# A graph-attention layer on one core: four overflow slots in place of seven, and seven more row tiles turned by VectorE instead of TensorE

## The chip, the cores and the metric

The kernel runs on one core of one Trainium2 chip. The metric is the device time of one launch in microseconds, and lower is better. The core's engines are TensorE (PE, matrix products), VectorE (DVE), ScalarE (ACT), GpSimd (POOL) and SyncE (SP); each takes its own instructions in the order in which they were queued. DMA queues belong to ScalarE, GpSimd and SyncE. PSUM is the memory that TensorE writes its results to.

## The reference

x is 2708 x 1024 in float32; adj is 2708 x 2708 with an edge at each place with chance 0.0014771, so a row has four edges on average. The weights are 1024 x 1024.

```
h   = relu(layernorm(x))
q   = h @ W_q.T + b_q;  k = h @ W_k.T + b_k;  v = h @ W_v.T + b_v
z   = (q @ k.T) / sqrt(1024) * adj
z   = where(z == 0, -10000, z)
out = x + relu(softmax(z, axis=1) @ v)
```

## The kernel before

**Two rewritings.** The kernel first forms M = W_q.T W_k / sqrt(1024), so that a score is (h_i M + b) . h_j and k is never formed. The values are summed as rows of h and multiplied by W_v afterwards. So there are two products of 2708 x 1024 by 1024 x 1024: the *q product* (h by M) and the *o product* (the weighted sums of rows of h by W_v). Only edges are scored and summed.

**Sorted tiles.** The 2708 rows are 22 tiles of 128 (the last has 20 rows). VectorE and ScalarE read adj, list up to 16 (`SLOTS`) neighbours of each row (`found`, `listed`) and count them (`counted`). Within tiles 0 to 7 and within tiles 8 to 21 the rows are sorted by their number of edges: `counts` prepares, `sort` has two small matmuls of TensorE, `put` writes the rows of the table `tab` to `tab_dram` in sorted order, and `reload` reads it back. From then on "tile t" is a sorted tile, and h is gathered by the table. Sorted tile t has K[t] slots, of which the first of each part (tiles 0 and 8, `HOSTS`) needs most, 15. Their first 8 (`WIDE`) slots stay with them; the rest goes to a shared spill tile (`SECOND`, number 21): its upper 64 partitions hold the slots 8 to 14 of the 64 longest rows of tile 0, its lower 64 those of tile 8, so `VK` is 7. The spill tile has scores and sums as a tile does; its sums go to `v_dram`, its sums of weights to `mass`, and each host adds them to its own (`m`, L904 on, and the last step of `sums`). Were a row longer than its slots, a general path at the end of the kernel would run.

**Units.** TensorE's work after M is a row of *units*: ten q pairs (units 0 to 9: tiles 0 and 1, 2 and 3, and so on), ten o pairs (units 10 to 19, in the order of the list `order`: tiles 6 and 5, 4 and 3, ...), and one single tile (`alone`, tile 8, the last of `order`). A pair of tiles is multiplied as a 2x2 block matrix with seven block products in place of eight. `blocks` (L711) makes the operands: a11, a12, a22 are transposed halves of the two row tiles; s1 = a22 + a21, s3 = a11 - a21, s2 = s1 - a11, s4 = a12 - s2 are sums of VectorE. `opened(n + 1)` issues unit n+1's products of a11 and of s1 inside unit n, ahead of unit n's last product (a22); `multiply(n, ...)` issues the other five and calls `after(0)` to `after(6)` between them. `after` is the place where all other work is put into the queues: unit n at step i is written (n, i).

**How a tile gets transposed.** In units up to 10 and in some later ones TensorE does it: `half_turned` (L415) makes four 128x128 transposes into PSUM, and ScalarE copies the half (L718) or VectorE uses it from PSUM. In the other way, called *faced* here, the rows are stored with the columns combed (ScalarE's copy L944 and a store to `u_dram`), read back by four quarter loads (`by_quarters`, L700), and VectorE turns 32x32 blocks in place (`faces`, L705); TensorE has no part in it. `faced_tiles` says which output tiles go this way:

```
if now < [unit - 2, 2] and unit <= len(q_pairs) + 4:
    faced_tiles.add(t)
```

that is, tiles whose sums are done early enough for their unit, in units up to 14. The single tile is transposed by TensorE (`turned`).

**The attention stream.** `attention` is a generator that hands out VectorE's long steps one by one, tile by tile in `order`, with the spill tile ahead of tile 0: `scores` (L863, one step for each slot: gathered rows of h times the rows of q, summed to one number), `weights`, and `sums` (L923, one step for each slot after the first; the first is an ACT copy, L912). `fill` queues gathers of h rows (L610, GpSimd) into eleven and later thirteen slots as they come free. `fetch` brings the q rows of a tile, called `pq`: for tiles 0 to 7 by a gather from `q_dram`, for the others by a plain load from `q_late` on SyncE's queue (L831, L833). `advance(share)` in `after` pulls some steps into VectorE's queue at each of the seven places of a unit; `share` (us by the kernel's own estimate of 1.3 for each long step) is 20.9/7, less 2.3/7 for each faced tile of the next unit.

**Order by hand.** `manual_schedule` fixes the order of ScalarE and VectorE (up to unit 3; after that VectorE's alone), and of GpSimd in two stretches. What goes where is written in `steps_at`, a list of short codes for each (unit, step): p = `counted` (ScalarE counts an adjacency tile), f and i = `found`, a = `apply` (normalise), k = `keep` (store h rows to `h_dram` and leave their sum for later), + = `owe` (four quarter additions of a tile to `hsum`, L298, on GpSimd), w = `put`, z and b = `reload`. The q pairs from unit 4 on gather their rows from `h_dram` (`load_rows`, "qr", L612); at (2, 5) the order in GpSimd's code is owe(8), owe(9), rows of unit 4, owe(10), owe(6), owe(7), rows of unit 5.

The functions that the diff touches, with the profile's line numbers:

## Time and profile before

| | before |
|---|---|
| median of 3 runs | 640.27 us (639.92 to 641.12) |
| the profiled execution's own time | 639.94 us |
| its span in the profile | 638.1 us |
| mean granted TensorE clock | 0.997 |
| busy: PE | 627.8 us (98%), 1651 instructions |
| busy: DVE | 522.4 us (82%), 1016 |
| busy: POOL | 360.2 us (56%), 383 |
| busy: ACT | 283.6 us (44%), 423 |
| moved by DMA | 176.96 MB, mean 277 GB/s |

The span is the time from the first to the last record of the profile; the execution's own time holds a little more. Busy time is what the profiler recorded for the engine's own instructions; a DMA that an engine issues is counted for the queue, except for the gathers and scatters of GpSimd, which have records of their own. In a row of the trace, "start duration engine line operation output<-inputs, shape" stand in this order, and the bracket at its end says how long the engine had been idle before it and what ended that.

### The profile page before, as it was taken

The page shows a single profiled execution, that of the slowest core. Times are in us where ns is not written, and L with a number is a line of the kernel's source. Part 1 is how long each engine was busy: PE and PEld are TensorE (multiplying, and loading weights), DVE is VectorE, ACT ScalarE, POOL GpSimd, SP SyncE. Part 2 cuts the span into 40 slices and gives each one's busy share as a digit, 9 for nine tenths or more (in the row PEclk, how much of TensorE's full clock was granted, in tenths as well). Part 3 has the DMA queues.
Part 4 walks back from the last instruction along what each step waited for, and adds up shares of the span by engine and source line. Part 5 has one row for each costly group of instructions (what it writes and reads, how often), then busy time and mean ns, then how long its engine had stood idle before and what let it go on. Part 6 is the DMA issues. An engine that isn't in the chain of part 4 may idle for free.

```text
span 638.1 us, 6156 instructions
## 1 busy us (share of the span) xinstructions
PE 627.8 (98%) x1651; PEld 317.9 (50%) x1651; DVE 522.4 (82%) x1016; ACT 283.6 (44%) x423; POOL 360.2 (56%) x383
## 2 busy tenths in 40 slices
PE   9999999999999999999999999999999999999994
PEld 5777766444444444444444444444444444444441
DVE  5999888997997625999888999999999889989121
ACT  3538985849667533424342144343342432333200
POOL 2639960885768357565651663476466878633311
PEclk9999999999999999999999999999999999999998
DMA  8999997598796439996798998999999999853631
GB/s 335 407 362 321 342 351 286 200 323 330 255 379 231 171 95 317 327 323 223 233 299 289 290 414 222 295 344 311 363 382 325 325 290 291 266 145 77 187 119 50
DMA packets 60192, 176.96 MB, mean 277 GB/s; under 512 B 9799, under 2 KB 15255, under 8 KB 59512
## 3 DMA queue, kind: packets, MB, share of 16 engines
q0 software_dynamic: 25136, 78.41, 39.4%
q1 hardware_dynamic: 29514, 78.61, 35.0%
q10 hardware_dynamic: 5502, 19.48, 7.8%
q8 instruction: 15, 0.25, 0.2%
q14 instruction: 25, 0.20, 0.1%
HBM read 145.65 MB, written 40.74 MB: 292 GB/s over the span
## 4 chain that ended last, share of the span: by engine, by line
PE 90%; issue 4%; POOL 2%; DMA 2%; DVE 1%; POOLq 0%; ACT 0%; ACTq 0%; DVEq 0%
PE ps L1010 40%; PE psy L1010 29%; PE ps_y L476 6%; PE ps_x L476 4%; PE ps_z L476 4%; PE pt L415 4%; POOL g L610 2%; DMA v_dram<-u 1%; DMA M<-h_dram,tab 1%; PE ps_y L511 1%; DVE junk L863 0%; PE ps_h L1218 0%; PE ps_v L594 0%; DVE u L923 0%; DVE s L722 0%
## 5 line engine op out<-in xcount | busy, mean ns | idle before, releaser
L610 POOL DMA_INDIRECT g<-h_dram,tab x94 | 120.2, 1278 | 79.9 <-DVE u L923 30.0
L1010 PE MATMUL psy<-wlow,s 128*128 128x512 f32 x320 | 144.0, 592 | 0.0
L1010 PE MATMUL ps<-M,a 128*128 128x512 f32 x320 | 144.0, 593 | 0.0
L863 DVE SCALAR_TENSOR_TENSOR junk<-g,pq 128x1024 uint8<-128x1024 f32 x93 | 113.8, 1224 | 13.4 <-DMA g<-h_dram,tab 10.4
L1010 PEld LDWEIGHTS ps<-M,a 128*128 128x128 f32 x320 | 59.7, 190 | 70.4 <-issue 69.1
L923 DVE SCALAR_TENSOR_TENSOR u<-g,coef,u 128x1024 f32<-128x1024 f32 x69 | 88.4, 1281 | 7.0 <-ACT u L912 5.8
L1010 PEld LDWEIGHTS psy<-wlow,s 128*128 128x128 f32 x320 | 59.6, 190 | 69.2 <-issue 69.0
L389 DVE FIND_INDEX8 at<-ones,adj 128x8 uint32<-128x685 f32 (+1 forms) x88 | 74.5, 864 | 0.0
L1010 PE MATMUL ps<-wlow,s 128*128 128x512 f32 x160 | 72.0, 593 | 0.4 <-DVE s L722 0.4
L1010 PE MATMUL ps<-M,s 128*128 128x512 f32 x160 | 72.1, 592 | 0.0
L1010 PE MATMUL psy<-wlow,a 128*128 128x512 f32 x160 | 72.0, 593 | 0.0
L368 ACT ACTIVATE sized<-adj 128x2708 uint8<-128x2708 f32 (+1 forms) x22 | 54.3, 2467 | 7.4 <-DMA adj<-in_adj_dram 6.1
L298 POOL TENSOR_TENSOR hsum<-hsum,x 128x256 f32<-128x256 f32 (+1 forms) x56 | 38.6, 732 | 26.2 <-DVE wlow L444 22.5
L1109 POOL DMA_INDIRECT y<-in_x_dram,tab x19 | 34.2, 1798 | 28.9 <-ACT y L1134 12.1
L1010 PEld LDWEIGHTS ps<-wlow,s 128*128 128x128 f32 x160 | 30.3, 190 | 38.9 <-issue 38.5
L1010 PEld LDWEIGHTS psy<-wlow,a 128*128 128x128 f32 x160 | 30.3, 190 | 38.5 <-issue 37.3
L1010 PEld LDWEIGHTS ps<-M,s 128*128 128x128 f32 x160 | 30.3, 190 | 38.1 <-issue 37.4
L808 POOL DMA_INDIRECT out_dram<-y,tab x21 | 27.4, 1306 | 32.0 <-DMA y<-in_x_dram,tab 15.8
L912 ACT ACTIVATE u<-g,coef 128x1024 f32<-128x1024 f32 x18 | 20.7, 1149 | 35.8 <-DVE coef L911 35.6
L276 ACT ACTIVATE x<-x,r 128x1024 f32<-128x1024 f32 (+1 forms) x22 | 25.9, 1232 | 6.6 <-POOL r L266 6.6
L722 DVE TENSOR_TENSOR s<-a,pt 128x512 f32<-128x512 f32 x30 | 19.2, 681 | 10.9 <-ACT a L718 10.9
L476 PE MATMUL ps_y<-wlow 128*128 128x512 f32 x64 | 27.6, 592 | 0.0
(251 smaller groups left out, 843.3 us busy)
## 6 DMA issues: line engine op xcount, KB each, us to landing
adj<-in_adj_dram SPq DMA_DIRECT2D x21, 1354.0 KB, 11.5
x<-in_x_dram SPq DMA_DIRECT2D x21, 512.0 KB, 8.2
h_dram<-x ACTq DMA_DIRECT2D x21, 512.0 KB, 7.4
q_late<-q SPq DMA_DIRECT2D x12, 512.0 KB, 5.1
pq<-q_late SPq DMA_DIRECT2D x12, 512.0 KB, 6.6
u_dram<-v ACTq DMA_DIRECT2D x10, 512.0 KB, 6.4
or<-u_dram SPq DMA_DIRECT2D x40, 128.0 KB, 7.0
M<-in_wv_dram SPq DMA_DIRECT2D x4, 1024.0 KB, 8.4
```

The source lines that it names most:

```text
L276: nc.scalar.activation(xs[i][:n], xs[i][:n], AF.Relu, bias=r[:n, 4, i:i + 1], scale=r[:n, 3, i:i + 1])
L298: small.append(nc.gpsimd.tensor_add(hsum[:n, cols], hsum[:n, cols], xt[:n, cols]))
L368: nc.scalar.activation(sized[:n], a[:n, :, :PW], AF.Abs, accum_out=total[:n, t:t + 1])
L389: nc.vector.max_index(at[:n, k - first_k, g, :], ones[:n, 0:8], a[:n, g, :])
L415: nc.tensor.transpose(pt[:, c, :], xt[:, k * P:(k + 1) * P], ident)
L476: mm = nc.tensor.matmul(bank, a_tile(o + H * a[0], a[1], i), b(o), start=first and o == 0, stop=(o == H - 1), skip_group_check=True)
L610: return nc.gpsimd.indirect_dma_start(out=dst, out_offset=None, in_=src, in_offset=off, bounds_check=N - 1, oob_is_err=False)
L808: to = nc.gpsimd.indirect_dma_start(out=out, out_offset=bass.IndirectOffsetOnAxis(ap=ptab.bitcast(U32)[:n, t, SLOTS:SLOTS + 1], axis=0), i ...
L863: chained(lambda: nc.vector.scalar_tensor_tensor(junk, g_of[t][s], 1.0, tq[t], op0=ALU.mult, op1=ALU.mult, accum_out=zall[:, t, s:s + 1]))
L923: chained(lambda: nc.vector.scalar_tensor_tensor(u, g_of[t][s], coef[:, s:s + 1], u, op0=ALU.mult, op1=ALU.add))
L1010: mm = nc.tensor.matmul(bank, a[:, c, :], b[:, c, :], start=False, stop=(c == 3), skip_group_check=True)
L1109: return nc.gpsimd.indirect_dma_start(out=y[:n], out_offset=None, in_=x, in_offset=off, compute_op=ALU.add)
```

## The change

The change has six parts.

1. **Four overflow slots.** `VK` is 4, and the spill tile holds each host's overflow in two pieces (`OVER`): for tile 0, slots 8 to 11 of its 48 longest rows on partitions 0 to 47 and slots 12 to 15 of its 8 longest on 48 to 55; for tile 8, 60 rows on partitions 56 to 115 and 12 on 116 to 127. The longer rows' second piece is added into the gathered first piece by an accumulating DMA, and `mass` has four columns.
2. **One q pair faced.** Pair 6 (`QFACED`, tiles 12 and 13) is gathered raw at (3, 3) into row tiles, combed by ScalarE and stored to `hq_dram` at (4, 2), and read back by quarters at (4, 3). (Steps are handed out by `after` at the end of a product, and the instructions' places in the engines' queues follow from the order lists and, for engines whose order is not fixed, from the scheduler.)
3. **More output tiles faced.** The condition admits units up to 15, and the units from 19 on and the single tile without regard to the time: pairs 5 and 9 of the output and tile 8. The single tile's rows are loaded at the end of unit 18 and turned by VectorE in one instruction.
4. **q rows by GpSimd.** The loads of `pq` from `q_late` are on GpSimd's queue.
5. **Load.** `share` is 22.0/7 before the last q unit, 18.2/7 in the two after that, 21.3/7 from there; the spill tile comes ahead of tile 3 instead of tile 0.
6. **Order.** At (2, 5) the rows of unit 4 are loaded ahead of all five `owe`; at (2, 3) the normalising and storing of tiles 8 to 10 comes ahead of counting p17; the second half's `put` is queued behind the last `root` of GpSimd instead of behind the last block product.

```diff
     HOSTS = (0, EARLY)
+    QFACED = (6,)
     SECOND = NT - 1
-    HP = P // 2
-    VK = K[0] - WIDE
-    assert K[0] == K[EARLY] and K[SECOND] == 0 and WIDE + VK <= SLOTS
+    VK = 4
+    OVER = ((48, 0), (8, 48)), ((60, 56), (12, 116))
...
-    mass = const.tile([P, 2], FT, name="mass")
+    mass = const.tile([P, 4], FT, name="mass")
+    nc.vector.memset(mass, 0.0)
...
-    for t in HOSTS:
-        nc.vector.memset(cap[:HP, t:t + 1], float(WIDE + VK))
+    for t, parts in zip(HOSTS, OVER):
+        for i, (rows, at) in enumerate(parts):
+            nc.vector.memset(cap[:rows, t:t + 1], float(WIDE + (i + 1) * VK))
...
             elif step[0] == "w":
-                with tc.issue_after((behind if first < EARLY else products)[-1].ins):
+                with tc.issue_after((behind if first < EARLY else rooted if first > EARLY else products)[-1].ins):
...
-        part = slice(HP, P) if lo >= EARLY else slice(0, HP)
-        loads.append((nc.gpsimd if lo >= EARLY else nc.sync).dma_start(
-            ptab[part, SECOND, 0:SLOTS + 1 - WIDE], src[0:HP, WIDE:SLOTS + 1]))
+        for i, (rows, at) in enumerate(OVER[lo >= EARLY]):
+            slot = WIDE + i * VK
+            loads.append((nc.gpsimd if lo >= EARLY else nc.sync).dma_start(
+                ptab[at:at + rows, SECOND, 0:SLOTS + 1 - slot], src[0:rows, slot:SLOTS + 1]))
+            if i and lo < EARLY:
+                loads.append(nc.sync.dma_start(ptab[at:at + rows, SECOND, SLOTS - WIDE:SLOTS + 1 - WIDE],
+                                               src[0:rows, SLOTS:SLOTS + 1]))
...
-                (2, 2): "p16", (2, 3): "p17 a8 k8 z", ...
+                (2, 2): "p16", (2, 3): "a8 k8 p17 z", ...
...
         if t == SECOND:
-            gather(tq[t][:HP], q_dram[:, :], t, SLOTS - WIDE, HP)
-            nc.sync.dma_start(tq[t][HP:], q_late[:HP, :])
+            rows = sum(rows for rows, at in OVER[0])
+            gather(tq[t][:rows], q_dram[:, :], t, SLOTS - WIDE, rows)
+            for rows, at in OVER[1]:
+                nc.gpsimd.dma_start(tq[t][at:at + rows], q_late[:rows, :])
         elif t >= EARLY:
-            nc.sync.dma_start(tq[t], q_late[(t - EARLY) * P:(t - EARLY + 1) * P, :])
+            nc.gpsimd.dma_start(tq[t], q_late[(t - EARLY) * P:(t - EARLY + 1) * P, :])
...
-            nc.sync.dma_start(mass[:HP, 1:2], mass[HP:, 0:1])
+            for c, (rows, at) in zip((1, 2, 3), (OVER[1][0], OVER[0][1], OVER[1][1])):
+                nc.sync.dma_start(mass[:rows, c:c + 1], mass[at:at + rows, 0:1])
...
+            if t in HOSTS and s == K[t] // 2 + 1:
+                rows, at = OVER[HOSTS.index(t)][1]
+                nc.gpsimd.dma_start(g_of[t][K[t]][:rows], v_dram[at:at + rows, :], accum_op=ALU.add)
...
-        if now < [unit - 2, 2] and unit <= len(q_pairs) + 4:
+        if now < [unit - 2, 2] and unit <= len(q_pairs) + 5 or unit >= len(units) - 1:
             faced_tiles.add(t)
...
-    stream = attention(order[:order.index(0)] + [SECOND] + order[order.index(0):])
+    stream = attention(order[:order.index(3)] + [SECOND] + order[order.index(3):])
...
+    def raw_rows(n):
+        raw_of[n] = [row_tile(f"raw_{t}") for t in units[n][1:]]
+        for xt, t in zip(raw_of[n], units[n][1:]):
+            gather(xt, h_dram[:, :], t, SLOTS, P)
+
+    def combed(n):
+        for i, xt in enumerate(raw_of.pop(n)):
+            v = row_tile(f"hv_{n}_{i}")
+            nc.scalar.copy(v.rearrange("p (a c r) -> p c a r", a=QUADS, r=QP),
+                           xt.rearrange("p (c a r) -> p c a r", a=QUADS, r=QP))
+            at = 2 * (n - QFACED[0]) + i
+            nc.scalar.dma_start(hq_dram[at * P:(at + 1) * P, :], v)
+
+    def quarter_rows(n):
+        rows_of[n] = [row_tile(f"qr_{t}") for t in units[n][1:]]
+        for i, xt in enumerate(rows_of[n]):
+            at = 2 * (n - QFACED[0]) + i
+            by_quarters(xt, hq_dram[at * P:(at + 1) * P, :])
...
-        share = 20.9 / 7
+        share = (22.0 if n < last_q else 18.2 if n < last_q + 2 else 21.3) / 7
...
             if (n, i) == (2, 5):
+                rows_of[FIRST] = load_rows(units[FIRST])
                 owe(8)
                 owe(9)
-                rows_of[FIRST] = load_rows(units[FIRST])
                 owe(10)
...
-                if i == (2 if n in (FIRST, last_q) else 4) and n + 2 > FIRST and n + 2 < len(units) and n + 2 not in rows_of:
+                if i == (2 if n in (FIRST, last_q) else 4) and n + 2 > FIRST and n + 2 < len(units) and n + 2 not in rows_of and n + 2 not in QFACED:
...
+            for step, at in ((raw_rows, {6: (3, 3)}), (combed, {6: (4, 2)}), (quarter_rows, {6: (4, 3)})):
+                for pair in QFACED:
+                    if at[pair] == (n, i):
+                        step(pair)
...
             if nxt is None and i == 1:
+                uT = work.tile([P, D], FT, tag="hT", name="T_alone", bufs=2).rearrange("p (c q) -> p c q", q=P)
+                faces(uT, single["rows"], 0, DC)
+                single["turned"] = uT
+            if n == len(units) - 2 and i == 6:
                 while alone not in done:
                     advance(1.0)
-                r, = load_rows(("o", alone))
-                single["turned"] = turned(r, "alone")
+                single["rows"], = load_rows(("o", alone))
```

17 lines of the change are left out of this document (12 added, 5 removed), and 2 rows, old and new, of the table steps_at.

## The prediction

> **What bounds the kernel now.** I read the page's table of engines first, then TensorE's own waits, then the chain that ended last.
>
> ```profile
> span 638.1 us, 6156 instructions
> PE 627.8 (98%) x1651; PEld 317.9 (50%) x1651; DVE 522.4 (82%) x1016; ACT 283.6 (44%) x423; POOL 360.2 (56%) x383
> ...
> PE ps_y L511 <- POOL hsum L121: 1.2, 1, 1.2
> PE ps L1010 <- DVE s L722: 0.4, 1, 0.4
> ...
> 597.38 0.87 PE pt L415 x8
> 629.41 0.70 DVE y_alone L1371
> ```
>
> TensorE is busy 627.8 of 638.1 us. It waits twice, 1.2 us for the first clear and 0.4 us for one sum of VectorE; its last matmul ends at 629.41, and the 8.7 us behind that are one addition, the last scatter and the end. So a TensorE instruction that is taken out is worth its full length, and any wait put before one costs its full length, because there is no slack in which to win it back. A turned tile is eight transposes of 128x128 and takes 0.87 us of the chain.
>
> **The change part by part. What TensorE loses.** Set side by side, the instruction orders of the two builds differ on TensorE by seven groups of eight transposes: the two tiles of q pair 6, four output tiles (pairs 5 and 9), the single tile. 7 x 0.87 = 6.1 us. The tail keeps its instructions.
>
> **What VectorE gets.** Fourteen half-tile turns (the single tile's two as one instruction), against three scores and three sums fewer, since the spill tile has 4 slots in place of 7.
>
> ```profile
> L863 DVE SCALAR_TENSOR_TENSOR junk<-g,pq 128x1024 uint8<-128x1024 f32 x93 | 113.8, 1224 | 13.4 <-DMA g<-h_dram,tab 10.4 <-DMA pq<-q_dram,tab 1.0 <-DMA pq<-q_late 0.2
> L923 DVE SCALAR_TENSOR_TENSOR u<-g,coef,u 128x1024 f32<-128x1024 f32 x69 | 88.4, 1281 | 7.0 <-ACT u L912 5.8
> L705 DVE STREAM_TRANSPOSE a<-or 128x512 f32<-128x512 f32 x15 | 10.0, 694 | 1.0 <-DMA or<-u_dram 1.0
> ...
> 388.19 0.69 DVE L722 TENSOR_TENSOR s<-a,s 128x512 f32<-128x512 f32 x1
> 389.03 3.67 PE L1010 MATMUL ps<-wlow,s 128*128 128x512 f32 x8 [0.36 <-DVE s L722]
> ```
>
> 14 x 0.69 = 9.7 us come, 3 x 1.22 + 3 x 1.28 = 7.5 us go. The tightest place is the sum s1 of unit 11, for which TensorE waited the 0.36 us above (389.03 is 0.84 after the sum's start; I use that hand-over below). Counted from unit 7's s1, where VectorE is paced by TensorE's transposes in both builds, to unit 11's, there are 71 scores and sums in the old order and 71 in the new, with the spill tile no longer followed at once by its sums. I take the 0.4 us as gone; at the worst it stays, or grows by the 2 us by which I may misjudge waits for ScalarE. Behind unit 11 the new order has fewer long steps in VectorE's queue in sum (6), so its lead grows.
>
> **The turned rows' round trip at the end.** Each newly turned output tile adds a copy on ScalarE, a store and four quarter loads. For the single tile this chain must fit between its last sum and TensorE's first use:
>
> ```profile
> 586.70 1.28 DVE L929 SCALAR_TENSOR_TENSOR u<-g,m,u 64x1024 f32<-64x1024 f32 x1
> 611.82 3.60 PE L1010 MATMUL ps<-M,T_alone 128*128 128x512 f32 x8
> ...
> L944 ACT COPY v<-u 128x1024 f32<-128x1024 f32 x10 | 10.5, 1046 | 22.6 <-DVE u L923 20.7 <-DMA g<-h_dram,tab 1.8
> u_dram<-v ACTq DMA_DIRECT2D x10, 512.0 KB, 6.4
> or<-u_dram SPq DMA_DIRECT2D x40, 128.0 KB, 7.0
> ```
>
> 1.05 + 6.4 + 7.0 + 1.4 for the turn is 16 us, and from 587.98 to 611.82 there are 24; cost 0, and if that cover failed, what is over 24. Moving the q loads of the late tiles from SyncE's to GpSimd's queue puts twelve loads in front of gathers. Both wait for steps of VectorE that lie one tile back, and VectorE holds gathered rows for about ten steps of 1.25 us ahead, against the 6.4 us in which its gathers land (median, quoted below): cost 0, at worst a few us of VectorE's lead.
>
> The Trainium skill speaks against this move: its page "SBUF — State Buffer" says under "SBUF: two separate sides" and in the box on the "DVE blocks DMA" trap that GpSimd writes the descriptors of its own DMAs through a port pair that VectorE can lock, and that SyncE's queue is free of that. By it each moved load could start one VectorE operation late. The gathers of this kernel are on the same queue:
>
> ```profile
> L610 POOL DMA_INDIRECT g<-h_dram,tab x94 | 120.2, 1278 | 79.9 <-DVE u L923 30.0
> ```
>
> 1278 ns on average with VectorE at 82%, against 0.94 of one at 206.62 (quoted below): the trace agrees in direction, with a third of a us each, 4 us of GpSimd's time over twelve loads and none of TensorE's.
>
> **The new wait at unit 4.** This is the step that I think decides. Early in unit 3's last third GpSimd gathers pair 6 raw (two gathers behind those of pair 5), ScalarE combs the rows into quarters, and they go out and back. In the built order ScalarE has the two comb copies *ahead* of the copy of unit 4's a22 out of PSUM, and GpSimd has all twenty quarter additions to hsum ahead of the gathers (before, eight of them came ahead of the first two gathers and filled a wait). ScalarE, VectorE and TensorE take their queues in order, so: raw gathers land -> two combs -> a22 -> s1 of unit 4 -> TensorE.
>
> ```profile
> 201.49 1.06 ACT L718 COPY a<-pt 128x512 f32<-128x512 f32 x2
> 205.69 0.58 ACT L718 COPY a<-pt 128x512 f32<-128x512 f32 x1 [3.14 <-PE pt L415]
> ...
> 206.45 1.27 DVE L722 TENSOR_TENSOR s<-a,pt 128x512 f32<-128x512 f32 x2
> ...
> 205.05 1.04 PE L415 MATMUL pt<-ident,qr 128*128 128x128 f32 x8
> 205.93 3.60 PE L1010 MATMUL ps<-M,a 128*128 128x512 f32 x8
> 209.36 3.60 PE L1010 MATMUL ps<-wlow,s 128*128 128x512 f32 x8
> 212.79 3.60 PE L1010 MATMUL psy<-wlow,a 128*128 128x512 f32 x8
> 216.23 1.02 PE L1010 MATMUL psy<-wlow,s 128*128 128x512 f32 x2
> ...
> 192.12 1.07 POOL L612 DMA_INDIRECT qr<-h_dram,tab  x1 [1.71 <-DMA h_dram<-x]
> 194.48 8.25 POOL L298 TENSOR_TENSOR hsum<-hsum,x 128x256 f32<-128x256 f32 x12
> 202.88 0.95 POOL L612 DMA_INDIRECT qr<-h_dram,tab  x1 [0.16 <-issue]
> 206.62 0.93 POOL L612 DMA_INDIRECT qr<-h_dram,tab  x1 [0.30 <-issue]
> ...
> DMA  0000006996095699995799989978510000000000
> qr<-h_dram,tab POOLq DMA_INDIRECT x4, 5.4
> DMA to landing us min/median/max: 4.3/6.4/8.0
> ```
>
> In the trace of before ScalarE is through with unit 4's first two copies at 202.55 and idles 3.14 us for the transposes; s1 starts at 206.45 and TensorE uses it at 209.36 without a wait. Now the new order. The first two gathers of q rows start at 192.12, when the sorted table and the stored rows have landed. The table's reload has the same instructions before it; its landing bounds this start, and I leave it at 192.1. The additions start 2.36 us later (194.48) and are 20 instead of 12: 20 x 8.25/12 = 13.75, so the four gathers start at 208.4. They follow each other by (206.62 - 202.88)/3 = 1.25, so the second raw one starts at 212.1. In the old trace the last of four started at 206.62 and the DMA engines fell silent in the slice before 212.0: 5.2 us. So the rows are there at 217.3. One comb (1.05 by the like copy above; the other runs while the second gather lands) ends at 218.4, a22's copy (0.58) at 219.0, s1 starts 0.18 later as before at 219.2, and TensorE gets it at 220.05. It stood ready at 209.36: **10.7 us** lost.
>
> **A second wait behind it.** VectorE's queue behind s1 holds the listing of the last adjacency rows and the counts whose result the small sorting matmul of TensorE needs.
>
> ```profile
> 208.48 0.91 DVE L1254 MEMSET g<- 128x1024 f32 x1 [0.16 <-issue]
> 216.81 0.31 DVE L666 TENSOR_TENSOR sort<-deg,down 128x144 bf16<-128x144 f32 x1
> ...
> 217.18 0.24 PE L678 MATMUL ps_in<-sort,before 128*128 128x144 bf16 x1
> ```
>
> From s1's start to the end of that step VectorE needed 217.12 - 206.45 = 10.67 us; one clear of a slot (0.91 + 0.16) has moved behind s1, so 11.74, until 230.95. TensorE reaches the sort two groups of 3.43 and four records of 0.43 later, 8.6 us, at 228.65 (one matmul later in its order than before), and waits again: **2.4 us**. The sorted table, and with it the attention steps, then move back with TensorE by the same 13 us, so nothing further is lost there, and nothing is regained.
>
> **Sum.** The profiled execution took 639.94, its span 638.1 plus 1.84 around it; the median of the three runs is 640.27, 0.33 above. 639.94 - 6.1 - 0.4 + 10.7 + 2.4 = 646.5; with the 0.33, **646.9**.
>
> Bounds of the first wait: a landing of 4.3 or 8.0 us in place of 5.2 makes it 0.9 less or 2.8 more. The start of the first q gathers could be earlier, because ScalarE now normalises tiles 8 to 10 ahead of one count over an adjacency row:
>
> ```profile
> 178.92 2.37 ACT L276 ACTIVATE x<-x,r 128x1024 f32<-128x1024 f32 x2 [1.36 <-POOL r L266]
> L368 ACT ACTIVATE sized<-adj 128x2708 uint8<-128x2708 f32 (+1 forms) x22 | 54.3, 2467 | 7.4 <-DMA adj<-in_adj_dram 6.1
> ```
>
> That is at most 2.47 + 1.36 = 3.8 us earlier for the stored rows; the table would then have to land earlier too. So 6.0 to 13.5 for the wait, and **642 to 651** for this case with 2.4 at the sort and the 0.4 kept or not.
>
> **Rivals.** *The plain gain.* The gathers land before ScalarE needs a22, or their wait is covered in a way I do not see: then only 6.1 + 0.4 are left, 633.8. For it: 6.1 us of a full engine go, and VectorE's balance holds. Against it: thirteen us of additions stand ahead of the gathers in an in-order queue, and a22's copy has 3 us to spare. It decides if the rows are there by about 208. Chance 0.15. *VectorE becomes the bound in the output units* (too little lead behind unit 11, or late q loads through GpSimd) besides the wait at unit 4: 2 to 6 us more, 649 to 653; against it the growing lead. Chance 0.08; without the wait at unit 4 it ends within 0.2% of before, together with a wait of half my size: 0.06. *The clock falls in the gap.*
>
> ```profile
> 629.40:638.00 8.60, 0.00 (x0) 0.00 (x0) 0.69 (x1) 0.00 (x0) 0.96 (x1) 0.75 0.15 56
> ```
>
> TensorE's granted clock is 0.75 over the last 8.6 us, in which it does nothing, so it drops to some half within such a gap. If the matmuls behind a gap of 10.7 us begin at half clock, eight records of 0.43 lose up to 3.4 us, of which 2.4 only replace the wait at the sort; about 1 us more, 648. No gap of that length lies inside the old span, so the rows cannot say how long a low clock lasts. The Trainium skill's page "TensorE: Matmul & The Clock Gate" (table of the two states) says that after an idle window of about 3.4 us the array runs at half clock until it has been busy for one. By that, 647.9 in place of 646.9; the 0.75 agrees with the drop. Chance 0.25, within the main case's range.
>
> **How the numbers follow.** The wait at unit 4 without the clock's price has 0.46, with it 0.25; then 0.15, 0.08 and 0.06. The likeliest gives 646.9. 638 to 652 leaves out the plain gain and a little above: 2 in 10. A measurement tells about 0.2%, 1.3 us, from no change. Faster 0.15; same 0.06; slower 0.46 + 0.25 + 0.08 = 0.79.
>
> **What would show it.** In the new profile: TensorE's waits list a wait for VectorE's s1 of about 10 us near 209 and one of about 2 us for the sort near 229; ScalarE idles from about 202.6 for a gather of raw; GpSimd's additions run in one block to about 208. TensorE has 56 transposes fewer, and its busy time falls by some 6 us less what a low clock adds. I am wrong if ScalarE's copy of unit 4's a22 ends by 208, if the gathers start before 205, or if TensorE's waits lie in the output units instead.

## The result and the profile after

| | before | after |
|---|---|---|
| median | 640.27 us (639.92 to 641.19, 5 runs) | 658.69 us (656.90 to 660.35, 5 runs) |
| the profiled execution, its span | 639.94, 638.1 us | 656.90, 655.2 us |
| TensorE busy, its own waits in all | 627.8, 1.6 us | 624.9, 20.5 us |
| mean granted TensorE clock | 0.997 | 0.982 |

The ratio is 1.0288, with a 95% interval of 1.0265 to 1.0311: 18 us slower. The forecast was 646.9 (638 to 652). Its direction was right; 11.8 us are missing from it. The table and the ratios below use executions in the fast state, and one of e8's ten, at 648.15 us, is left out as slow.

The page of the changed kernel, its engines and the granted clock in 40 slices:

```profile
span 655.2 us, 6119 instructions
PE 624.9 (95%) x1595; PEld 313.3 (48%) x1595; DVE 523.0 (80%) x1023; ACT 284.7 (43%) x419; POOL 367.8 (56%) x397
...
PEclk9999999999999699999999989999999999999998
```

What its TensorE waited for (us in total, times, longest):

```profile
PE ps L1028 <- DVE s L731: 15.6, 2, 13.0
PE ps L1028 <- ACT psy L1041: 2.6, 1, 2.6
PE ps_y L516 <- POOL hsum L124: 1.2, 1, 1.2
...
PE ps_in L687 <- DVE sort L675: 0.2, 1, 0.2
```

TensorE has 56 instructions fewer, as built. Where it stood is seen in its timeline (start, us, then the instruction, and behind it the idle time before it and what ended that); the clock's two low slices, the 14th and the 24th, lie at the same two places:

```profile
205.61 3.60 PE L1028 MATMUL ps<-M,a 128*128 128x512 f32 x8
222.25 5.54 PE L1028 MATMUL ps<-wlow,s 128*128 128x512 f32 x8 [13.04 <-DVE s L731]
...
233.15 0.24 PE L687 MATMUL ps_in<-sort,before 128*128 128x144 bf16 x1 [0.21 <-DVE sort L675]
...
380.36 3.67 PE L1028 MATMUL ps<-wlow,s 128*128 128x512 f32 x8 [2.57 <-DVE s L731]
386.59 3.57 PE L1028 MATMUL ps<-M,a 128*128 128x512 f32 x4 [2.56 <-ACT psy L1041]
```

The start of each unit's s1 product, after minus before, dates every gain and loss: -0.3 us up to unit 3; +12.9 at unit 4 and +15.1 at unit 5 (the wait, and eight matmuls that took 5.54 in place of 3.60); 1.75 back at unit 6, whose tiles TensorE no longer transposes; level at +13.4 to unit 9; **+16.1 at unit 10 and +19.9 at unit 11**, a second loss of 6.5; 2.0 back at unit 15, 1.8 at unit 19; +16.0 at the single tile and +17.1 at the end, 1.1 of it behind the last matmul. The first loss was forecast, the second was not.

The first loss in the timelines of the changed kernel; ScalarE:

```profile
201.17 1.06 ACT L727 COPY a<-pt 128x512 f32<-128x512 f32 x2
218.75 2.24 ACT L1240 COPY hv<-raw 128x1024 f32<-128x1024 f32 x2 [16.51 <-DMA raw<-h_dram,tab]
...
220.89 0.58 ACT L727 COPY a<-pt 128x512 f32<-128x512 f32 x1
```

VectorE:

```profile
221.50 1.28 DVE L731 TENSOR_TENSOR s<-a,pt 128x512 f32<-128x512 f32 x2 [15.24 <-ACT a L727]
```

GpSimd:

```profile
195.81 13.73 POOL L303 TENSOR_TENSOR hsum<-hsum,x 128x256 f32<-128x256 f32 x20
...
213.47 0.95 POOL L617 DMA_INDIRECT raw<-h_dram,tab  x1 [0.30 <-issue]
```

Twenty additions, then the raw gathers, then two combs, then a22's copy, then s1: the chain of the prediction, instruction by instruction.

The second loss: VectorE stood 6.5 us for a block of W_v at the first of the four differences (`T[:, 0] = b12 - b11`), with s1 of unit 10 queued behind it:

```profile
373.12 2.29 DVE L1305 TENSOR_TENSOR wlow<-M 128x2048 f32<-128x2048 f32 x1 [6.52 <-DMA M<-in_wv_dram]
```

SyncE's queue shows why the block came late:

```profile
361.27 0.34 SPq L1102 DMA_DIRECT2D q_late<-q  x1
361.71 0.38 SPq L1301 DMA_DIRECT2D M<-in_wv_dram  x1
```

In the built order the load of b11 stands behind the store of unit 8's second q tile, which waits for unit 8's last product. The load's target was free from 353.6 on (the start of unit 9's s1 product, which follows the last use). In the kernel before the load stood ahead of that store and went out at 340.43, 0.2 us after the same event.

### The profile page after: what moved, and what is told of

Read it like the earlier page. It is cut to its first block, busy times and chain, and to the rows that moved or that the text cites. A ratio compares the mean times of both kernels' runs of the same rounds, so it can differ in the third digit from the quotient of the medians.

```text
span 655.2 us, 6119 instructions
## 1 busy us (share of the span) xinstructions
PE 624.9 (95%) x1595; PEld 313.3 (48%) x1595; DVE 523.0 (80%) x1023; ACT 284.7 (43%) x419; POOL 367.8 (56%) x397
## 4 chain that ended last, share of the span: by engine, by line
PE 42%; DVE 11%; DMA 8%; issue 4%; ACT 1%; POOL 1%; SPq 0%; POOLq 0%; ACTq 0%; DVEq 0%
PE ps L1028 23%; PE psy L1028 17%; DVE u L939 4%; DVE junk L874 3%; DMA pq<-q_late 2%; DMA g<-h_dram,tab 2%; DVE s L731 1%; DMA or<-u_dram 1%; PE pt L420 1%; DMA q_late<-q 1%; DMA raw<-h_dram,tab 1%; DMA u_dram<-v 1%; DVE g L1296 1%; DVE u L1143 0%; DVE a L714 0%
## 5 line engine op out<-in xcount | busy, mean ns | idle before, releaser
L1028 PE MATMUL ps<-M,a 128*128 128x512 f32 x320 | 146.0, 598 | 2.6 <-ACT psy L1041 2.6
L615 POOL DMA_INDIRECT g<-h_dram,tab x92 | 115.8, 1259 | 56.3 <-issue 17.4
L874 DVE SCALAR_TENSOR_TENSOR junk<-g,pq 128x1024 uint8<-128x1024 f32 x91 | 111.3, 1224 | 18.6 <-DMA g<-h_dram,tab 14.9
L939 DVE SCALAR_TENSOR_TENSOR u<-g,coef,u 128x1024 f32<-128x1024 f32 x72 | 92.3, 1281 | 5.7 <-ACT u L925 4.0
L1028 PE MATMUL ps<-wlow,s 128*128 128x512 f32 x160 | 73.9, 606 | 15.6 <-DVE s L731 15.6
L731 DVE TENSOR_TENSOR s<-a,pt 128x512 f32<-128x512 f32 x24 | 15.4, 681 | 23.9 <-ACT a L727 23.9
L962 ACT COPY v<-u 128x1024 f32<-128x1024 f32 x15 | 15.7, 1045 | 38.1 <-DVE u L939 36.2
L925 ACT ACTIVATE u<-g,coef 128x1024 f32<-128x1024 f32 x16 | 18.4, 1148 | 29.9 <-DVE coef L924 29.9
L769 ACT COPY ps<-bp_sb 128x512 f32<-128x512 f32 x42 | 24.6, 596 | 10.6 <-DVE y L1164 9.9
```

The source lines that it names most:

```text
L615: return nc.gpsimd.indirect_dma_start(out=dst, out_offset=None, in_=src, in_offset=off, bounds_check=N - 1, oob_is_err=False)
L731: step = (eng or nc.vector).tensor_tensor(ops[name], a, b, op=op)
L769: nc.scalar.copy(return_[h], row[:, h * NB:(h + 1) * NB])
L874: chained(lambda: nc.vector.scalar_tensor_tensor(junk, g_of[t][s], 1.0, tq[t], op0=ALU.mult, op1=ALU.mult, accum_out=zall[:, t, s:s + 1]))
L925: nc.scalar.activation(u, g_of[t][0], AF.Copy, scale=coef[:, 0:1])
L939: chained(lambda: nc.vector.scalar_tensor_tensor(u, g_of[t][s], coef[:, s:s + 1], u, op0=ALU.mult, op1=ALU.add))
```

## The experiments

Two theories. **Q:** two misplaced queue entries (the combs on ScalarE, the W_v load on SyncE) make the two losses, and moving each one removes its loss. **V:** VectorE, or what feeds it, is the real limit around units 9 to 11, so that removing one wait there uncovers another. Times of different groups of runs are compared by their ratio to the kernel before, which ran beside each group (640.2 to 643.2 us). The executions of one kernel spread over several microseconds (e8's from 638.39 to 647.21), and a trace is of one of them: e3's and e14's are of their longest, e18's of one 3.6 us below its median. So waits read from a trace need not add up to the difference of the medians.

| run | median, us | ratio to before (95%) |
|---|---|---|
| e1 combs behind a22 | 648.72 | 1.0130 (1.0097 to 1.0163) |
| e2 W_v load ahead of the q store | 657.00 | 1.0265 (1.0239 to 1.0292) |
| e3 both | 648.20 | 1.0108 (1.0086 to 1.0131) |
| e4 no faced q pair | 647.07 | 1.0103 (1.0082 to 1.0125) |
| e5 e3, q loads on SyncE | 652.78 | 1.0149 (1.0097 to 1.0200) |
| e6 e1, pace as before | 642.87 | 1.0000 (0.9976 to 1.0024) |
| e7 e1, pace lower | 644.92 | 1.0017 (0.9993 to 1.0041) |
| e8 e7, additions as before | 642.03 | 0.9987 (0.9951 to 1.0024) |
| e9 after, pace as before | 654.10 | 1.0221 (1.0201 to 1.0241) |
| e10 tiles and slots, all orders as before | 657.49 | 1.0274 (1.0261 to 1.0287) |
| e11 e10 without the q pair | 655.98 | 1.0257 (1.0236 to 1.0278) |
| e12 before, five late tiles turned | 644.59 | 1.0080 (1.0062 to 1.0099) |
| e13 e6, additions as before, faster late pace | 643.22 | 1.0041 (1.0024 to 1.0059) |
| e14 e10, spill tile early | 648.75 | 1.0119 (1.0096 to 1.0142) |
| e15 e12, faster late pace | 646.68 | 1.0099 (1.0077 to 1.0122) |
| e16 before, pairs 5 and 9 turned | 641.95 | 1.0027 (1.0009 to 1.0046) |
| e17 before, q pair 6 turned | 642.66 | 0.9980 (0.9957 to 1.0002) |
| e18 before, pair 5 turned | 645.95 | 1.0034 (1.0010 to 1.0059) |

**The two queue entries: e1, e2, e3, e4.**

```diff
 e1 (acted holds ScalarE's u2 copies, from multiply)
-                        step(pair)
+                        with tc.issue_after(acted[-1].ins) if step is combed else nullcontext():
+                            step(pair)
 e2 (the entry (0, 0) of the W_v list is left out; in between(n), behind opened(n + 1):)
+            if n + 1 == last_q:
+                nc.sync.dma_start(M[:, 0, 0], of_wv(0, 0))
 e3: both
 e4
-    QFACED = (6,)
+    QFACED = ()
```

> The changed kernel, but ScalarE's two comb copies of pair 6 (and their stores) are queued behind its copy of unit 4's u2, so behind unit 4's a22, instead of ahead of it. Theory (the queue order makes the wait): the 13.0 us wait of TensorE for s1 of unit 4 goes, and with it 1.9 us of matmuls at a low clock behind it and 0.2 us at the sort; 656.9 becomes about 641.8. The gathers still land at about 219, so the combs end near 222 and the quarter rows are there long before unit 6 needs them. Rival A (the gathers behind the twenty additions are late for something else too, such as the rows of unit 5 or of unit 6): a wait of several us shows up in unit 5 or 6, and the time stays above 647. Rival B (VectorE has lost its lead and TensorE only waits later): less than 10 us come back, with waits for VectorE in units 8 to 14.

> The changed kernel, but the load of the first block of W_v into M's first block is queued on SyncE ahead of the store of unit 8's second q tile instead of behind it. Theory (that store waits for unit 8's last product, so the load starts 8 us after its target is free, and VectorE stands 6.5 us at the difference that needs it): VectorE's wait goes, TensorE's two waits of 2.6 us each in units 9 and 10 go with the 1.2 us of slow matmuls behind them; 656.9 becomes about 650.6; the wait at unit 4 stays. Rival (VectorE is overloaded in the last q unit and the first output units): at least 3 us of the waits of TensorE stay there though VectorE no longer waits for the load, and the time is 653 or more.

> Both edits at once: the comb copies behind unit 4's a22, and the first block of W_v loaded ahead of the q store. If the two waits are all that the change added, 656.9 - 15.1 - 6.3 = 635.5, faster than before by about 4.5 us (6.1 us of transposes gone, with some 1 us more at the end of the span). Rival (VectorE's lead is too small once TensorE no longer stands still): waits for VectorE's sums in units 11 to 19, and a time from 637 to 645.

> The changed kernel without its faced q pair: pair 6 is transposed by TensorE as before; all else as changed, the twenty additions still in one block ahead of the second two gathers. Theory: no comb stands ahead of unit 4's a22, so the 13.0 us and 2.1 us behind them go; sixteen transposes come back (1.75 us): 656.9 - 15.1 + 1.75 = 643.5, and the waits in units 9 and 10 stay. Rival (the additions ahead of the gathers are enough to make unit 5's rows late): a wait of TensorE for the transposes or sums of unit 5, and 647 or more.

What TensorE waited for in e1:

```profile
PE ps L1027 <- ACT psy L1040: 5.6, 1, 5.6
PE ps L1027 <- DVE s L731: 2.1, 1, 2.1
PE ps_in L687 <- DVE sort L675: 1.7, 1, 1.7
```

And in e3:

```profile
PE psy L1027 <- DVE wlow L1306: 9.0, 1, 9.0
PE ps_in L687 <- DVE sort L675: 2.5, 2, 2.0
```

The wait of 13 us at unit 4 is gone in e1, e3 and e4: theory Q holds there, and the combs ahead of a22 are its cause. But e1 came to 648.7, not 641.8. The sort's wait came out at 1.7 us (its cause is below), and the loss in units 9 to 11 grew. Unit 11's s1 stood at +1.4 (unit 9), +3.8 (unit 10), +12.0 against before: 10.6 us, where after had lost 6.5. e2 tells the same story. The W_v load went out in time and VectorE did not wait for it any more; TensorE stood 5.65 us for the next difference instead, VectorE having waited 5.85 us for q rows; units 9 to 11 lost 6.6 us, as in after, and the time fell by 0.2%, which lies inside the two intervals, and not by 1%. In e3 VectorE's timeline names what had been hidden behind the load:

```profile
377.16 1.22 DVE L874 SCALAR_TENSOR_TENSOR junk<-g,pq 128x1024 uint8<-128x1024 f32 x1 [6.83 <-DMA pq<-q_late]
...
378.31 0.69 DVE L1113 TENSOR_TENSOR q<-ps,u 128x512 f32<-128x512 f32 x1
378.91 2.28 DVE L1306 TENSOR_TENSOR wlow<-wlow 128x2048 f32<-128x2048 f32 x1
```

GpSimd issued the load that it waited for 14 us earlier, behind a gather of 4.83 us:

```profile
358.24 4.83 POOL L615 DMA_INDIRECT g<-h_dram,tab  x1 [0.30 <-issue]
363.08 0.61 POOL L844 DMA_DIRECT2D pq<-q_late  x1
```

VectorE stands for the q rows of tile 17. Behind that score in its queue are an addition that frees a PSUM bank (ScalarE's copy psy waits for that, and TensorE for the copy) and the difference of W_v's second block. Tile 17's q rows are the ones that unit 8 has only just formed. So theory V fits here in a form of its own: not too much work, but the wrong work in front. In after VectorE had waited only 0.5 us for these rows, since W_v's block held it up first. In the order of the kernel before, the first score of tile 17 came behind all four differences.

**Whose fault the place is: e5, e6, e7, e8, e9.**

```diff
 e5 (on e3)
-            nc.gpsimd.dma_start(tq[t], q_late[...])      and the two of the spill tile
+            nc.sync.dma_start(tq[t], q_late[...])
 e6 (on e1), e9 (on after)
-        share = (22.0 if n < last_q else 18.2 if n < last_q + 2 else 21.3) / 7
+        share = 20.9 / 7
 e7 (on e1)
+        share = (20.0 if n < last_q else 20.9) / 7
 e8 (on e7): at (2, 5) owe(8), owe(9) ahead of load_rows(units[FIRST]) again
```

> e3 (combs behind a22, W_v block ahead of the q store) with the q loads of the late tiles back on SyncE's queue. In e3 VectorE stood 6.8 us for the q rows of tile 17, with the difference for W_v's second block and an addition of unit 9 queued behind that score, and TensorE stood 9.0 us for the difference. Theory (pace: the scores of tile 17 come in VectorE's queue ahead of work that TensorE needs, and its q rows have only just been formed): on SyncE the load stands behind eight quarter loads of unit 11's rows, which end near 370 as in e3, so its rows land near 377 either way; the wait stays within 2 us of e3's, and the time within 3 us of e3's 648.2. Rival (GpSimd's queue makes it late: the load stood there behind nine gathers and took 14.0 us to land against 6.6 on SyncE before): the wait shrinks by 5 us or more and the time falls below 643.

> e1 (combs behind a22) with the pace of the attention stream as before the change: share 20.9/7 in every unit. In VectorE's queue the first score of tile 17 then stands behind the difference for W_v's second block instead of ahead of it, and on SyncE the load of W_v's first block stands ahead of unit 8's second q store again, as it did before the change. Theory (pace): TensorE's waits of 2.1 and 5.6 us in units 9 and 10 go with some 2 us of slow matmuls: 648.7 becomes about 639.5; a wait of some us at the third and fourth differences may be left, since tile 17 is still scored ahead of them. Rival (VectorE has too much work in these units whatever the pace): waits of 4 us or more for VectorE in units 9 to 12, time 645 or more.

> e1 with share 20.0/7 in the q units and 20.9/7 after them: with three scores and three sums fewer the stream then stands where it stood before the change when the W_v differences are due, and the scores of tile 17 come fifteen rows behind the second difference. Theory (pace): no wait of TensorE in units 9 to 11; 648.7 - 10.4 = 638.3, with the 1.7 us at the second sort left. Rival (the stream is then too late for the output units): waits in units 12 to 19 for sums or rows, 641 or more.

> e7 with GpSimd's order at (2, 5) as before the change: eight of the twenty additions ahead of the first two gathers of q rows, twelve behind. In e1 and e4 VectorE's sum s2 of unit 4 took 2.2 and 2.7 us instead of 0.68 and ended 0.6 us behind the last of GpSimd's twenty additions; the small sort then waited 1.7 and 2.05 us. Theory (that sum cannot run beside the additions, and the late block of them is the cause): with the additions done by about 203 the sum takes 0.68 us again, the sort waits 0 to 0.6 us, and the time is 1.5 us below e7's, near 636.8, with at least 3 us less than before. Rival (the wait at the sort is the clear that moved behind s1): the sort still waits over 1 us, time as e7.

> The changed kernel with nothing undone but the pace of the attention stream: share 20.9/7 in every unit as before the change; the comb copies still stand ahead of unit 4's a22. Theory (the two costs are independent and add): e6 against e1 showed the pace to cost about 9 us; 656.9 - 10 = 647, with the wait of 12 to 13 us at unit 4 and 2 us of slow matmuls behind it left, and no wait of more than 3 us in units 9 to 11. Against the kernel before that is 6 to 7 us slower, which is what the prediction summed without the pace. Rival (the delay at unit 4 gives GpSimd and the DMAs time, so that the two costs overlap): 651 or more, or waits in units 9 to 11 of 5 us and more.

e5's one large wait, in TensorE's timeline:

```profile
381.13 2.08 PE L1027 MATMUL ps<-M,a 128*128 128x512 f32 x2 [12.22 <-ACT psy L1040]
```

The waits above half a microsecond in e6's TensorE timeline, units 9 to 11:

```profile
382.67 3.70 PE L1027 MATMUL psy<-wlow,s 128*128 128x512 f32 x8 [0.73 <-ACT u L1071]
...
391.92 3.67 PE L1027 MATMUL ps<-wlow,s 128*128 128x512 f32 x8 [2.11 <-DVE s L731]
```

And in e9's, the only one at that place:

```profile
382.54 3.70 PE L1027 MATMUL psy<-wlow,a 128*128 128x512 f32 x8 [0.37 <-DVE q L1108]
```

What the pace moves is seen in e6. VectorE's second difference and, behind it, the first score of tile 17:

```profile
363.81 2.28 DVE L1304 TENSOR_TENSOR wlow<-wlow 128x2048 f32<-128x2048 f32 x1
...
370.06 1.23 DVE L874 SCALAR_TENSOR_TENSOR junk<-g,pq 128x1024 uint8<-128x1024 f32 x1 [2.17 <-issue]
```

And on SyncE's queue, the load of W_v's first block and the store of unit 8's second q tile:

```profile
340.14 0.35 SPq L1300 DMA_DIRECT2D M<-in_wv_dram  x1
...
347.62 0.34 SPq L1101 DMA_DIRECT2D q_late<-q  x1
```

GpSimd's queue alone is not the cause: on SyncE the load went out later still, at 370.5 us behind quarter loads, and the wait was 12.2 us, 3.2 more than in e3, outside the 2 expected. The pace is. With 20.9/7 the large wait is gone, with e1's combs (e6: 1.0130 to 1.0000) and without them (e9: 1.0288 to 1.0221). The pace moves two things at once: the first score of tile 17 goes behind the second difference, and the load of W_v's first block goes ahead of unit 8's second q store again. e2 and e3 show that the load alone is not enough; the score alone was not tried. My expectation for e9 (647) was 7 us too low. In units 9 to 11 the pace was worth about the same with the stop at unit 4 (6.5 us lost in after, 0.1 in e9) and without it (10.6 in e1, 3.2 in e6). By its trace e9 lost the rest elsewhere: against after, 1.3 us ahead of unit 4, 1.8 at unit 17 and 1.4 at the end. Why is open.

e7 went lower with the pace and found no more: VectorE did not wait for tile 17's rows, but 3.7 us for W_v's third block. e8 is half a success. Its first half is about the sort. e1's VectorE:

```profile
207.55 2.17 DVE L731 TENSOR_TENSOR s<-s,a 128x512 f32<-128x512 f32 x1
```

e1's GpSimd:

```profile
195.40 13.76 POOL L303 TENSOR_TENSOR hsum<-hsum,x 128x256 f32<-128x256 f32 x20
```

e8's VectorE:

```profile
209.79 0.68 DVE L731 TENSOR_TENSOR s<-s,a 128x512 f32<-128x512 f32 x1
```

e8's GpSimd:

```profile
196.06 8.24 POOL L303 TENSOR_TENSOR hsum<-hsum,x 128x256 f32<-128x256 f32 x12
```

With the additions done earlier VectorE's s2 took 0.68 us again and not 2.17. But TensorE still stood 1.54 us at the sort; VectorE had waited 5.1 us for an adjacency tile in that execution. My theory of the sum held, the gain did not come. e10 and e13 below have the same order of additions: s2 took 0.69 and 0.68 us there, and TensorE did not wait at the sort.

**What the tiles are worth with the old orders: e10, e11, e14.**

```diff
 e10 (on after): e1's edit; share = 20.9 / 7; the spill tile ahead of tile 0; q loads on SyncE;
     owe(8), owe(9) ahead of load_rows; "p17 a8 k8 z"; the table's put behind products
 e11: e10 with QFACED = ()
 e14: e10 with
-    stream = attention(order[:order.index(0)] + [SECOND] + order[order.index(0):])
+    stream = attention(order[:order.index(3)] + [SECOND] + order[order.index(3):])
```

> All seven tiles turned by VectorE and the four slots, but every order as before the change: combs behind a22, pace 20.9/7, spill tile ahead of tile 0, q loads on SyncE, eight additions ahead of the first q gathers, p17 ahead of a8. Theory (the tiles are worth 6.1 us and what the change lost came from orders): the waits at the sort and at unit 4 are gone; 1 to 3 us of waits for VectorE are left in units 10 and 11 where it now also scores tile 17 ahead of the third difference; 3 to 5 us faster than before. Rival (the added stores and quarter loads and VectorE's turns cost as much as the transposes did): within 2 us of before.

> e10 without the faced q pair: the four slots, and the five output tiles turned by VectorE (40 transposes fewer than before, 4.35 us). Theory: 4.35 us less the same waits in units 10 and 11 as e10: 2 to 3 us faster than before, about 1.7 us slower than e10. Rival (the q pair's extra traffic of a store and eight quarter loads delays the loads of W_v): faster than e10.

> e10 with the spill tile ahead of tile 3 as in the change, everything else as in e10. In e10 VectorE stood 7.8 us in unit 9 for the accumulated second piece of the spill tile, with the W_v differences and s1 of unit 10 behind it. Theory (two DMAs one behind the other need about 20 us from the spill tile's store, which the place ahead of tile 0 does not give): the 7.8 us wait goes, TensorE's waits of 11 us in units 10 and 11 shrink to 3 or less, 657.5 becomes about 645. Rival (q loads on SyncE's queue, which stand behind stores and quarter loads there, make those waits): 652 or more, with VectorE waiting for q rows of tile 17.

e10 was to show the gain and was as slow as after. e11, without the q pair, has an interval that overlaps e10's, so neither of its two readings is borne out. VectorE in e10:

```profile
361.83 1.27 DVE L946 SCALAR_TENSOR_TENSOR u<-g,m,u 48x1024 f32<-48x1024 f32 x1 [7.80 <-DMA g<-v_dram]
```

GpSimd in e10:

```profile
353.25 0.96 POOL L938 DMA_DIRECT2D g<-v_dram  x1 [6.14 <-DMA g<-v_dram]
```

What VectorE waited for in e14, one row of that view:

```profile
DVE junk L874 <- DMA pq<-q_late: 8.3, 2, 7.5
```

The spill tile's second piece is added by a DMA that waits for the first piece's; GpSimd stood 6.1 us at it, and the sum landed 8.6 us after its issue. Ahead of tile 0 the spill tile comes too late for that, so its early place belongs to the four slots. With it (e14) 1.0274 became 1.0119: the wait at the spill tile is gone. TensorE still stands 5.2 us in unit 10, and VectorE waits there for q rows that SyncE's queue brought. That suggests that the move of the q loads to GpSimd, too, belongs to this change, but no run moves these loads alone in this order. Both of e14's readings were half right.

**The end of the kernel, and single pairs: e12, e15, e13, e16, e17, e18.**

```diff
 e12 (on before): the condition, the load at (18, 6) and the turn of the single tile, as in the change
 e15 (on e12)
+        share = (20.9 if n < last_q + 2 else 21.8) / 7
 e13 (on e6): owe(8), owe(9) first, and
+        share = (20.9 if n < last_q + 2 else 21.6) / 7
 e16, e18 (on before)
-        if now < [unit - 2, 2] and unit <= len(q_pairs) + 4:
+        if now < [unit - 2, 2] and unit <= len(q_pairs) + 5 or unit == len(units) - 1:     (e16)
+        if now < [unit - 2, 2] and unit <= len(q_pairs) + 5:                               (e18)
 e17 (on before): QFACED, hq_dram, raw_rows, combed, quarter_rows as in the change, with e1's edit
```

> The kernel before with one edit: the two output tiles of pair 5, those of pair 9 and the single tile are turned by VectorE (40 transposes fewer), seven slots, pace and orders untouched. Theory (VectorE has room behind unit 12, and the round trip of the single tile is covered): 4.35 us faster, less a wait of 1 to 3 us at the single tile, whose turned rows came 2.0 and 3.0 us late in e7 and e8: 1.5 to 4.4 us faster than before. Rival (ten more half-turns delay the stream so that the last sums are late): no gain, with waits of TensorE behind unit 17.

> e12 (the kernel before, five late tiles turned by VectorE) with a share of 21.8/7 from unit 11 on in place of 20.9/7. In e12 TensorE stood 4.15 us for the single tile, whose last sum ended at 598.2 where the kernel before had it at 588.0, because every turned tile of the next unit takes 2.3/7 off the share. Theory: eight units of 0.9 bring the last sum some 7 us earlier, the wait at the single tile goes with the slow matmuls behind it (5.9 us together), and the 4.35 us of transposes show: 1 to 4 us faster than before. Rival (VectorE cannot run faster there, as the gathers set its pace): the wait stays above 2 us and the time above before's.

> e6 (combs behind a22, pace as before in the q units) with eight of GpSimd's additions ahead of the first q gathers again, and a share of 21.6/7 from unit 11 on, so that the last sums come earlier. Theory (what e6 lost of the 6.1 us is 1.5 at the sort, 3 in units 10 and 11, and 1 to 2 at the end): the sort's wait and the single tile's go, 2 to 3 us below e6's ratio of 1.000, so 0.995 to 0.997 of before. Rival (GpSimd's wait for the two pieces of the spill tile, 11.8 and 9.2 us in e6 with gathers queued behind it, holds the late gathers, and a higher share only moves VectorE's wait): no change against e6.

> The kernel before with only the four output tiles of pairs 5 and 9 turned by VectorE (32 transposes fewer, 3.5 us), the single tile by TensorE as before. Theory: no store and quarter loads behind the last sum, so no wait at the single tile of over 1 us unless the sum itself comes too late: it may end up to 10 us later than before (588.0) and the row load needs about 7, so 604 at the latest against the first transpose at 597.2; a wait of up to 7 us is possible, and without it 2 to 3 us faster than before. If the time is slower than before and the wait is there, the late sums and not the turning cost the time.

> The kernel before with one edit: q pair 6 is gathered raw, combed by ScalarE (its copies queued behind unit 4's u2), stored, and read back by quarters; seven slots, pace, queues and all output tiles as before. Sixteen transposes fewer, 1.75 us. Theory (the raw gathers cost nothing where nobody waits for them, and the pair's rows are there 40 us ahead): 1.2 to 1.75 us faster, 0.997 to 0.998 of before, with no new wait of over 0.5 us at unit 4, at the sort or in unit 6. Rival (the four 0.7 us turns come out of VectorE's lead and the tightest place, s1 of unit 11, pays): TensorE's wait of 0.36 us there grows to 1.5 us or more, and the time is within 0.2% of before.

> The kernel before with one edit: the two output tiles of pair 5 (unit 15) are turned by VectorE. Sixteen transposes fewer, 1.75 us. In e12, e15 and e16, which hold this pair, TensorE lost about 0.8 us to the wait for s1 of unit 11 (0.9, 0.5 and 1.2 against 0.36 us) and 0.5 to 1.5 us to a copy of ScalarE in unit 15. Theory: those come along, and 0 to 1 us is left, 0.998 to 1.000 of before. Rival (they came from pair 9 and the single tile): 1.75 us faster, without these waits.

e12's last sum and its turn, on VectorE:

```profile
596.91 1.28 DVE L929 SCALAR_TENSOR_TENSOR u<-g,m,u 64x1024 f32<-64x1024 f32 x1
...
612.71 1.25 DVE L705 STREAM_TRANSPOSE T_alone<-or 128x1024 f32<-128x1024 f32 x1 [13.45 <-DMA or<-u_dram]
```

e12's TensorE, which waits for the turn:

```profile
614.01 5.40 PE L1010 MATMUL ps<-M,T_alone 128*128 128x512 f32 x8 [4.15 <-DVE T_alone L705]
```

VectorE's waits for gathers in e15:

```profile
DVE junk L863 <- DMA g<-h_dram,tab: 17.1, 4, 7.3
```

TensorE in e16:

```profile
597.94 1.06 PE L415 MATMUL pt<-ident,u 128*128 128x128 f32 x8 [2.28 <-DVE u L929]
```

The round trip of the single tile takes 14.5 us from the sum to the turn, as forecast, but its sum now ends at 598.2 and not at 588.0. The pace gives up 2.3/7 for each turned tile of the next unit, and pairs 5 and 9 are four of them; e18, with pair 5 alone, ended that sum at 596.7. That this share is the cause is not shown, for a faster late pace did not help by itself (e15: that sum runs from 596.77 for 1.27 us, and VectorE waits 17.1 us for gathers in place of before's 10.4). TensorE stands 4.15 us in e12 and pays 1.8 more for slow matmuls. In e13 the same remedy did move the sum, with four slots and the spill tile early: it ended at 587.9, where e6 had 596.6. TensorE did not stand at the single tile in either. The time was lost in other places, 1.9 us with slow matmuls behind it in unit 16, and was not below before. In e16 the last sum was as late as in e12, and the transposes stood 2.28 us for it. e18's trace shows its 1.75 us lost to a ScalarE copy in unit 15 (1.29 us: it stood behind a step that waited for an addition of VectorE) and to rows that came 2.1 us late in unit 3, which the edit does not touch; why its median is 3.6 us above this execution is open. e17 is the only single edit with some gain left over, 0.2% (interval 0.9957 to 1.0002), which the measurement does not tell from none; in its trace TensorE stands 1.7 us for rows in unit 3 and 2.1 us for VectorE in unit 10. No version was shown to be faster than the kernel before.

## Why the prediction was right or wrong

The profiled execution took 656.90 us and its sum said 646.5. Of these 10.4 us about 7 come from the step on VectorE, about 2 from unit 4 and the sort, and about 1.5 from the turned tiles and the end; the median lies another 1.8 above the profiled execution, where 0.3 was forecast.

- **TensorE's loss of 6.1 us**: right for 5.5 us. 56 instructions fewer; 1.75 at unit 6, 2.0 at unit 15 and 1.8 at unit 19 are seen directly. The single tile's 0.87 does not show: TensorE waited 0.56 us for a copy of ScalarE in its place. Behind the last matmul 1.1 us came on top, whose cause is open.
- **The new wait at unit 4**: right in every link, and mis-sized: 13.04 against 10.7 us. The additions took 13.73 us (13.75 forecast) but began at 195.81, not at 194.48, and the last rows landed 6.4 us after their gather started, not 5.2, at about 219.9 (217.3). The first comb ran during that landing, as forecast. The range of 6.0 to 13.5 held it. e1 and e4 show the cause.
- **The clock in the gap**: the rival with 0.25 happened. Eight matmuls took 1.94 us more, and the sort's wait shrank from the 2.4 forecast to 0.21, as that rival had it: 15.2 us in all against 14.1. Where TensorE did not stand for s1, it waited 1.70 (e1) and 2.05 us (e4) at the sort, but 1.49 and 1.99 of these are another cause, a slow s2 (below).
- **What VectorE gets**: this step failed. "71 scores and sums in the old order and 71 in the new" was the wrong question: by the traces the counts are equal (71 from unit 6's s1 on, 56 from unit 7's, which the prediction names). "I take the 0.4 us as gone" priced the change of pace at nothing. What mattered was which step stood where: the first score of tile 17, whose q rows had just been formed, had moved ahead of an addition and a difference that TensorE waits for, and W_v's first load had moved behind a q store. TensorE lost 6.5 us here in after and 10.6 in e1, where 0.4 was to be won, and the pace alone takes this away (0.1 left in e9, 3.2 in e6).
- **The transfers of SyncE**: the same step left out that the load of W_v's first block had gone behind a q store. It was the wait that after showed, 6.5 us of VectorE. Loaded in time it won little (e2: 0.2%), because the q rows of tile 17 were late anyway.
- **q loads through GpSimd, cost 0**: not refuted: e5 and e14 speak against putting them back, and no run tries the queue alone on the kernel before. The Trainium skill's page "SBUF — State Buffer", under "SBUF: two separate sides", warns that a load issued by GpSimd may have to wait for VectorE. No run singles that out; an issue took 0.56 to 0.63 us on GpSimd in after and 0.32 to 0.47 on SyncE in e5, and what stood ahead in each queue cost more.
- **The single tile's round trip, cost 0 with 24 us of cover**: right in after, where the turn was done at 625.2 for a use at 627.8, but with 17.3 us of cover and not 24. The cover was taken from the old trace, and the change shortens it; it was 11.7 us in e12, where the wait and the slow matmuls cost 5.9 us. In e6 and e13 it cost nothing.
- **Bounds of the range**: the upper end, 652, took the main case's own spread and gave VectorE's part 2 to 6 us with a chance of 0.08, on the ground of "the growing lead". The size was near (6.5), the place was not: that rival spoke of the units behind unit 11 and of late q loads through GpSimd, and the loss lay in units 9 to 11. A change of a pacing number deserved a rival of its own. (The main case's own terms add up to 650.1 at the most, not to 651.)

## What to carry to other kernels

Where engines take queues in order, do not count the work between two points; list what stands directly ahead of each instruction that the bound engine waits for, before and after, and ask of each of these when its own data arrives. Here a wait that was removed showed the next one behind it (W_v's block, then the q rows, then W_v's next block), so price a queue entry by taking it away in a run and not by its wait in one trace. A cover read from the old trace has to be read again with the change in it.

## What the runs showed of the hardware

- VectorE's s2, whose two operands both lie in SBUF, took 2.17 and 2.67 us in e1 and e4, and 0.68 in e8. In e1 and e4 it ended 0.55 us after GpSimd's last addition (209.16 and 209.72 in e1). The sums just ahead of it, with one operand in PSUM, ran beside the additions at 0.64 us each. The Trainium skill's page "SBUF — State Buffer" states this under "SBUF: two separate sides": the port pair that GpSimd and VectorE share is an exclusive lock, which a VectorE operation with two SBUF inputs needs against a GpSimd operation that reads SBUF. The runs agree, and the prediction did not ask it of the twenty additions.
- After a gap of 13.04 us eight matmuls took 1.94 us more than 3.60, and after one of 2.95 us (e8, at the single tile) 1.80 more, and after ones of 1.92 us in e13 and 2.30 us in e11 they also took 5.40; after the gap of 2.57 us in the changed kernel they took 3.67, and after one of 3.64 us in e8 3.70. The Trainium skill's page "TensorE: Matmul & The Clock Gate", under "What's actually happening", puts the limit at an idle window of about 3.4 us; the runs differ from that, since gaps below it were followed by slow matmuls in one place and not in another, and one above it by none. Why is left open.
